# Idle bf16 products on TensorE behind each pair of edge tiles of a two-layer graph attention kernel, with a reordered start, shared edge pools and a different ending

## The chip, the cores and the metric

The kernel runs on one core of a Trainium2 chip. The metric is the time of one execution on the device in microseconds (us). The number to be forecast is the median of several runs of the changed kernel; the kernel before has a median of 2784.78 us.

## What is computed

The reference is a graph network with 6250 nodes and 100000 edges, which come sorted by destination. Cut to what matters:

```python
h = relu(layernorm(x))                      # x: 6250 x 768, no scale and shift
h = relu(gat(h, W1, heads=4))               # 768 -> 4 x 64
h = relu(gat(h, W2, heads=1))               # 256 -> 256
h = relu(h @ Wm1 + bm1)                     # 256 -> 256
out = x + h @ Wm2 + bm2                     # 256 -> 768

def gat(h, W, heads):                       # edges and one self loop per node
    h = h @ W
    e = leaky_relu((h*a_src).sum()[src] + (h*a_dst).sum()[dst], 0.2)
    w = exp(e - max over the edges of dst)
    return sum over edges of w*h[src]  /  sum over edges of w   (+ bias), by dst
```

## The kernel before

**Stages.** There are 49 node tiles of 128 nodes (the last has 106), and the edges lie in 196 groups of 4 tiles of 128 edges, of which 782 tiles hold edges. The work goes through three stages.

1. *Features* (lines 193 to 273). For each node tile SyncE loads x and its transpose (`fetch`, two transfers of 384 KB), VectorE takes mean and variance (`moments`), TensorE spreads the mean over the array with one float32 product (`spread_means`), VectorE and ScalarE subtract and apply relu (`centre`), TensorE multiplies with W1 in six float32 products (`features1`), and `keep1` writes a row of 264 numbers per node to `table1` in device memory.
2. *Edges of layer 1* (`layer_edges`, line 317). For each tile of 128 edges GpSimd issues an indirect DMA that gathers 128 rows of `table1` into `G` (`gather`, line 339), ten groups ahead, into a pool of twelve groups. `make_mask` compares destination numbers, which `fetch_rows` loads broadcast to all partitions (512 KB per 16 tiles), with the partition number; `meet` multiplies this mask (bf16) with the destination scores (`e_ps`). `pair` then takes two tiles: two exponentials on ScalarE, three or four operations on VectorE that end in `hw`, and two float32 products of 128 x 128 by 128 x 260 (258 in layer 2) on TensorE that sum the edges of a group into a window of 128 destinations (`o_ps`, line 429). `gather_up` adds the window to the running sum `acc`, from which a copy of 32 rows per group fills the sum of a node tile. Once a node tile is full its generator `node.steps` is put on the list `late`, and `advance`, called after each pair, makes one step of it: in layer 1 the division, two transposes, the product with W2 and a row of `table2`.
3. *Edges of layer 2*, the same function with another node program (`Node2.steps`): division, transposes, the product with Wm1, that with Wm2 in two halves (`y_ps`), the sum with x + bm2, and the write of the result.

**Order.** The order of each engine's instructions is that of the program text, since these parts stand in `manual_schedule`. Of the main loop:

```python
for g in range(NG):
    gather(g + AHEAD); pair(g, 0); advance(); make_hot(g + 1)
    ...                                   # join / fetch_rows, meet, make_mask
    pair(g, 1); advance(); gather_up(g - 1)
```

The layers run one after the other: a gather of layer 2 may read any row of `table2`, so the first waits for the last row that layer 1 writes.

**PSUM.** The eight banks hold the counter `iota_ps` (1), tag "e" (2), tag "n" (2) and tag "o" (3, the windows `o_ps`).

**Partial tile.** The last node tile has 106 rows. Its load of x (line 156), its reload in layer 2 (line 608) and its write of the result (line 651) are each one transfer of 106 rows. Line 617 adds bm2, broadcast to all partitions, to x. Lines 455 and 458 copy the last window into the last sum.

Of the kernel before, what the change touches and what calls it, by code (L numbers as in the profile page):

```python
# [17 lines left out]
P = 128  # L18
# [3 lines left out]
HID = 256  # L22
# [25 lines left out]
def kernel(  # L48
# [39 lines left out]
    make_identity(nc, ident)  # L88
    iota = const.tile([P, P], F32, name="iota")
# [18 lines left out]
    for k in range(4):  # L108
        nc.vector.memset(keep[32 * k:32 * k + 32, k:k + 1], 0.0)

# [32 lines left out]
    def scores_in(ps, w, wt, a, K, H):  # L143
        p = ps.tile([P, K, 2 * H], F32, name="aps", tag="e")
        for k in range(K):
            for j in range(KH):
                nc.tensor.matmul(p[:, k], wt[:, j, k * P:(k + 1) * P], a[:, j],
                                 start=(j == 0), stop=(j == KH - 1))
        nc.vector.tensor_copy(w[:, :, HID:], p)

    def load_x(xp, i):
        n = min(P, N - i * P)
        t = xp.tile([P, IN_DIM], F32, name="xt", tag="xt")
        if n < P:
            nc.vector.memset(t, 0.0)
        nc.sync.dma_start(t[:n], x[i * P:i * P + n])
        return t, n
# [4 lines left out]
    def edge_places(ones):  # L162

        dst_i = ones.tile([P, NET], I32, name="dst_i")
        nc.scalar.dma_start(dst_i, dst_cols)
        dri = ones.tile([NCH, CH], I32, name="dri")
        nc.scalar.dma_start(dri, dst_rows)
        nc.scalar.dma_start(src_i, src_cols)
        for layer in bT:
            with nc.allow_non_contiguous_dma(reason="256 numbers"):  # L170
                nc.scalar.dma_start(bT[layer], {1: b1, 2: b2}[layer].rearrange("(k p) -> p k", p=P))
        yield

        drm = ones.tile([NCH, CH], BF16, name="drm")
        for d, n, w, to, f in ((dst_i, P, NET, dcol, dst_f), (dri, NCH, CH, drm, None)):
            m = ones.tile([n, w], I32, name=f"m{n}")
            nc.vector.tensor_scalar(m, d, P - 1, None, ALU.bitwise_and)
            yield
            if f is None:
                f = ones.tile([n, w], F32, name=f"f{n}")  # L180
            nc.vector.tensor_copy(f, d)
            yield
            far = ones.tile([n, w], F32, name=f"far{n}")
            nc.vector.tensor_scalar(far, f, float(N), 256.0, ALU.is_ge, ALU.mult)
            yield
            nc.vector.tensor_add(to, far, m)
            yield
        nc.scalar.dma_start(dmod_d, drm)
# [3 lines left out]
    bT = {layer: const.tile([P, KH], F32, name=f"bT{layer}") for layer in (1, 2)}  # L192
    with tc.tile_pool(name="w1p", bufs=1) as wp, tc.tile_pool(name="x1", bufs=6) as xp, \
            tc.tile_pool(name="wk1", bufs=3) as wk, tc.tile_pool(name="once", bufs=1) as ones, \
            tc.manual_schedule():
        xs, xTs, means, cents, rs = {}, {}, {}, {}, {}

        def fetch(i):
            xs[i], _ = load_x(xp, i)
            xTs[i] = xp.tile([P, KI, P], F32, name="xTt")  # L200
            nc.sync.dma_start(xTs[i], xT[i].rearrange("p (k n) -> p k n", k=KI))

        def moments(i):
            xt = xs.pop(i)
            stats = wk.tile([P, 2, nc.vector.BN_STATS_DIM], F32, name="stats")
            for j in range(2):
                nc.vector.bn_stats(stats[:, j], xt[:, j * 384:(j + 1) * 384])  # L207
            mv = wk.tile([P, 2], F32, name="mv")
            nc.vector.bn_aggr(mv, stats)
            std = wk.tile([P, 1], F32, name="std")  # L210
            nc.scalar.activation(std, mv[:, 1:2], AF.Sqrt, bias=eps_c)
            rstd = wk.tile([P, 1], F32, name="rstd", bufs=4)
            means[i] = mv, std, rstd

        def spread_means(i):
            mv, _, rstd = means[i]
            m_ps = ps.tile([P, P], F32, name="mean_ps", tag="n")
            nc.tensor.matmul(m_ps, mv[:, 0:1].to_broadcast([P, P]), ident, start=True, stop=True)
            means[i] = m_ps, rstd
# [9 lines left out]
        def features1(i):  # L229
            r, rstd = rs.pop(i)  # L230
            h_ps = ps.tile([P, HID + 8], F32, name="h_ps", tag="o", bufs=3)
# [14 lines left out]
        fetch(0)  # L246
        loaded = weights_in(wp, W1T, A1, KI, 4, "w1")
        fetch(1)
        w1 = wp.tile([P, KI, HID + 8], F32, name="w1")
        nc.sync.dma_start(w1[:, :, :HID], W1.rearrange("(k p) f -> p k f", p=P))  # L250
        for i in range(2, 5):
            fetch(i)
        pieces = edge_places(ones)
        next(pieces)
        for i in range(-3, NT):
            if i == 0:
                scores_in(ps, w1, *loaded, KI, 4)
            if 0 <= i:
                if i + 5 < NT:
                    fetch(i + 5)  # L260
                h = features1(i)
            if i + 3 < NT:
                moments(i + 3)
            if 0 <= i + 2 < NT:
                _, std, rstd = means[i + 2]
                nc.vector.reciprocal(rstd, std)
                spread_means(i + 2)
            if 0 <= i + 1 < NT:
                centre(i + 1)
            if 0 <= i:  # L270
                keep1(i, *h)
                if i >= 2:
# [43 lines left out]

    def layer_edges(layer, H, node, pre, matched):
# [3 lines left out]
        with tc.tile_pool(name=f"g{layer}", bufs=AHEAD + 2) as gp, \  # L321
                tc.tile_pool(name=f"rows{layer}", bufs=3) as rows, \
                tc.tile_pool(name=f"eg{layer}", bufs=2) as eg, \
# [3 lines left out]
            G, drow, mask, hot, e_ps, o_ps = {}, {}, {}, {}, {}, {}  # L327
# [5 lines left out]
            def gather(g):  # L333
                if not 0 <= g < NG:
                    return
                G[g] = gp.tile([P, TPG, TW[layer]], F32, name="G")
# [5 lines left out]

            def fetch_rows(r):

                k = 16 * r
                if 0 <= k < NET:
                    drow[r] = rows.tile([P, 16 * P], BF16, name="drow")
                    n = min(16, NET - k) * P
                    nc.sync.dma_start(drow[r][:, :n], bcast(dmod_d, n, k * P))
# [5 lines left out]
            def make_mask(u):  # L355

                if not 0 <= u < NU:
                    return
                a, b = (t * P for t in both(u))
                mask[u] = eg.tile([P, 8 * P], BF16, name="mask")  # L360
                at = u % 2 * 8 * P
                nc.vector.tensor_scalar(mask[u][:, a:b], drow[u // 2][:, at + a:at + b], pidx, None,  # L362
                                        ALU.is_equal)

# [29 lines left out]
            def pair(g, p):  # L394
# [26 lines left out]
                if g not in o_ps:  # L421
                    o_ps[g] = ps.tile([P, RW[layer]], F32, name="o_ps", tag="o", bufs=3)
                for t in range(2):
# [3 lines left out]
                    else:  # L427
                        l, r = hot[g][:, k], hw[:, t].rearrange("p h c -> p (h c)")
                    nc.tensor.matmul(o_ps[g], l, r[:, :RW[layer]], start=(k == tiles(g)[0]),  # L429
                                     stop=(k == TPG - 1))  # L430

            done, run, late = {}, {}, []

            def gather_up(g):
# [3 lines left out]
                acc = sums.tile([P, RW[layer]], F32, name="acc")  # L438
                if g == 0:
                    nc.vector.tensor_copy(acc, o_ps.pop(g))  # L440
                else:
                    nc.vector.scalar_tensor_tensor(acc, run[0], keep[:, (g + 1) % 4:(g + 1) % 4 + 1],  # L442
                                                   o_ps.pop(g), ALU.mult, ALU.add)
                run[0] = acc
                a = g - 2
                if a < 0:
                    return
                t, q = divmod(a, 4)
                if q == 0:
                    done[t] = sums.tile([P, RW[layer]], F32, name="sum", bufs=3)  # L450
                    node.prefetch(t)
                if q == 2:
                    node.ahead(t)
                r = slice(32 * q, 32 * q + 32)
                nc.scalar.activation(done[t][r], acc[r], AF.Copy)  # L455
                if g == NG - 1:
                    node.ahead(t)
                    nc.vector.tensor_copy(done[t][64:], acc[64:])
                    q = 3
                if q == 3:  # L460
                    late.append(node.steps(t, done.pop(t)))
# [7 lines left out]
            for r in range(3):  # L469
                fetch_rows(r)  # L470
            for u in range(2):
                make_mask(u)
# [6 lines left out]
            for g in range(NG):  # L479
# [7 lines left out]
                else:  # L487
                    if g % 4 == 0:
                        fetch_rows(g // 4 + 3)
# [6 lines left out]
                hot.pop(g, None)  # L496
            gather_up(NG - 1)
# [18 lines left out]
    with tc.tile_pool(name="w2p", bufs=1) as wp, tc.tile_pool(name="wk2", bufs=2) as wk:  # L516
        w2 = with_scores(ps, wp, W2, W2T, A2, KH, 1, "w2")

        class Node1:
# [12 lines left out]
            def steps(self, t, sum_):  # L532
# [13 lines left out]
                for k in range(KH):  # L546
                    nc.tensor.matmul(h_ps, rT[:, k], w2[:, k], start=(k == 0), stop=(k == KH - 1))
# [7 lines left out]
        with tc.tile_pool(name="pre1", bufs=1) as pre:  # L555
            pre1 = prepare(pre, 1, 4)
            with tc.manual_schedule():
                layer_edges(1, 4, Node1(), pre1, lambda: None)


    with tc.tile_pool(name="wmp", bufs=1) as wp, tc.tile_pool(name="x3", bufs=3) as xp, \
            tc.tile_pool(name="wk3", bufs=2) as wk, tc.tile_pool(name="pre2", bufs=1) as pre, \
            tc.manual_schedule():
# [3 lines left out]
        bm2b = wp.tile([P, OUT_DIM], F32, name="bm2b")  # L567
# [4 lines left out]
        def matched():  # L572
# [6 lines left out]
            nc.scalar.dma_start(bm2b, bcast(bm2, OUT_DIM))  # L579
# [20 lines left out]
        class Node2:  # L600
            rows, xs = {}, {}

            def prefetch(self, t):
# [4 lines left out]
                nc.sync.dma_start(self.xs[t][0][:n], x[t * P:t * P + n])  # L608
# [6 lines left out]
            def ahead(self, t):  # L615
                xt, n = self.xs[t]
                nc.vector.tensor_add(xt[:n], xt[:n], bm2b[:n])

            def steps(self, t, sum_):
# [23 lines left out]
                for s in range(2):  # L643
                    y_ps[s] = ps.tile([P, half], F32, name="y_ps", tag="n")
                    for j in range(KH):
                        nc.tensor.matmul(y_ps[s], mT[:, j], wm2[:, j, s * half:(s + 1) * half],  # L646
                                         start=(j == 0), stop=(j == KH - 1))
# [3 lines left out]
                nc.sync.dma_start(out[t * P:t * P + n], y[:n].rearrange("p s f -> p (s f)"))  # L651
# [301 lines left out]
```

## Time and profile before

| | us |
|---|---|
| median of 3 runs | 2784.78 (2783.95 to 2788.01) |
| the profiled execution, its own time | 2218.71 |
| its span, first to last instruction | 2216.9 |
| PE (TensorE products) busy | 1581.7 |
| DVE (VectorE) busy | 1480.5 |
| POOL (GpSimd) busy | 1518.4 |
| ACT (ScalarE) busy | 599.4 |
| first gather of layer 1 starts, from the span's start | 187.83 |
| first gather of layer 2 starts | 1186.64 |
| last gather of layer 2 starts | 2184.07 |

Read it so: the profile is of one execution, which was much shorter than the runs that were timed (2218.71 against 2784.78 us); every duration below is of that one execution. A group's line gives line number, engine, operation, output and inputs, count, then busy time, mean ns of one, and the idle time of the engine ahead of it with what ended it. "PEclk" and the clock column are the share of TensorE's full clock that was granted. A float32 product appears as two records.

### The profile page before, as it was taken

Reading aid. Unit: us, or ns where it says so; the run is one execution under the profiler, and the core shown is the slowest. Engines: PE = TensorE matmul, PEld = TensorE weight load, DVE = VectorE, ACT = ScalarE, POOL = GpSimd, SP = SyncE. Lnnn points to the kernel's source line nnn. Section 1 sums busy time; section 2 is a strip of 40 time slices with the busy share of each in tenths; the row PEclk is TensorE's granted clock in tenths of the full one; section 3 lists DMA queues with packets and bytes.
Section 4 is the critical chain, followed back from the end, with each engine's and each line's share of the span. In section 5 each row is a group of like instructions: output and inputs, shape, how many; then the busy total and the mean of one; then the engine's idle time right before and its main releaser. Section 6 shows DMA issues by size and latency. Waiting matters only on the chain. (4 is left out here: it accounts for less than half of the span.)

```text
span 2216.9 us, 25764 instructions
## 1 busy us (share of the span) xinstructions
PE 1581.7 (71%) x6588; PEld 1099.4 (50%) x6589; DVE 1480.5 (67%) x4510; ACT 599.4 (27%) x2602; POOL 1518.4 (68%) x1672
## 2 busy tenths in 40 slices
PE   7995766676667676666675777677877777777776
PEld 6783444444444444444443455555555554555553
DVE  6665677777777677777775666666666666666663
ACT  3552222222222222222222222222222222222221
POOL 0004777777777777777775777777777777777773
PEclk9997777877887877887886798888777878778786
DMA  8893555555555555545545565565556556555652
GB/s 288 291 306 109 143 145 151 151 139 148 152 152 141 146 151 151 150 139 150 151 122 172 162 182 158 183 182 165 177 181 182 166 174 183 171 166 182 181 143 89
DMA packets 149839, 370.16 MB, mean 167 GB/s; under 512 B 34354, under 2 KB 60978, under 8 KB 149684
## 3 DMA queue, kind: packets, MB, share of 16 engines
q0 software_dynamic: 75072, 209.10, 35.0%
q1 hardware_dynamic: 72052, 156.47, 21.3%
q10 hardware_dynamic: 2560, 2.86, 0.4%
q8 instruction: 56, 0.92, 0.2%
q14 instruction: 99, 0.81, 0.1%
HBM read 335.80 MB, written 32.50 MB: 166 GB/s over the span
## 5 line engine op out<-in xcount | busy, mean ns | idle before, releaser
L339 POOL DMA_INDIRECT G<-table,src_i x1564 | 1504.4, 962 | 496.1 <-issue 404.8
L429 PE MATMUL o_ps<-hw,hot 128*128 128x260 f32 x1564 | 590.8, 514 | 319.0 <-DVE hw L418 310.9
L429 PE MATMUL o_ps<-G,hw 128*128 128x258 f32 x1564 | 564.2, 497 | 260.2 <-DVE hw L413 255.9
L429 PEld LDWEIGHTS o_ps<-hw,hot 128*128 128x128 f32 x1564 | 345.1, 244 | 503.8 <-DVE hw L418 436.2
L429 PEld LDWEIGHTS o_ps<-G,hw 128*128 128x128 f32 x1564 | 339.2, 238 | 425.5 <-DVE hw L413 371.7
L406 DVE TENSOR_TENSOR e_ps<-e,e_ps 128x8 f32<-128x8 f32 (+1 forms) x782 | 129.6, 166 | 550.9 <-ACT e L403 550.8
L455 ACT ACTIVATE sum<-acc 32x260 f32<-32x260 f32 (+1 forms) x388 | 161.7, 417 | 696.7 <-DVE acc L442 695.5
L413 DVE TENSOR_SCALAR hw<-iota_ps,dcol,w 128x128 f32<-128x128 f32 x782 | 285.0, 406 | 14.4
L401 ACT ACTIVATE e<-G 128x8 f32<-128x8 f32 (+1 forms) x782 | 158.9, 203 | 471.1 <-DMA G<-table,src_i 452.1
L418 DVE TENSOR_TENSOR hw<-G,e_ps 128x520 f32<-128x520 f32 x391 | 271.8, 695 | 14.5 <-DVE e_ps L416 1.2
L442 DVE SCALAR_TENSOR_TENSOR acc<-acc,keep,o_ps 128x260 f32<-128x260 f32 (+1 forms) x390 | 185.7, 476 | 3.3 <-PE o_ps L429 3.3
L233 PE MATMUL h_ps<-w,r 128*128 128x264 f32 x588 | 146.5, 401 | 13.2 <-ACT r L226 13.1
L403 ACT ACTIVATE e<-G 128x8 f32<-128x8 f32 (+1 forms) x782 | 150.0, 192 | 0.2
L646 PE MATMUL y_ps<-wm,mT 128*128 128x384 f32 x392 | 143.1, 488 | 1.3 <-ACT mT L640 0.9
L372 DVE TENSOR_TENSOR hot<-iota_ps,dcol 128x512 f32<-128x512 f32 (+1 forms) x196 | 133.8, 682 | 0.0
L233 PEld LDWEIGHTS h_ps<-w,r 128*128 128x128 f32 x588 | 112.2, 197 | 33.5 <-ACT r L226 15.5
L243 POOL COPY row<-sd 128x4 f32<-128x4 f32 x49 | 9.1, 186 | 170.0 <-ACT sd L242 170.0
L512 ACT ACTIVATE rT<-tp,bT 128x128 f32<-128x128 f32 x196 | 61.2, 363 | 159.6 <-PE tp L505 159.3
L362 DVE TENSOR_SCALAR mask<-drow,pidx 128x1024 bf16<-128x1024 bf16 (+1 forms) x196 | 96.4, 493 | 2.2 <-DMA drow<-dmod_d 2.2
L383 PEld LDWEIGHTS <-mask 128*128 128x128 bf16 x1564 | 73.3, 101 | 42.6 <-issue 18.4
L646 PEld LDWEIGHTS y_ps<-wm,mT 128*128 128x128 f32 x392 | 74.2, 190 | 34.1 <-ACT mT L640 1.4
L207 DVE BATCH_NORM_STATS2 stats<-xt 128x6 f32<-128x384 f32 x98 | 49.9, 551 | 51.0 <-DMA xt<-in_x 50.4
(385 smaller groups left out, 1091.4 us busy)
## 6 DMA issues: line engine op xcount, KB each, us to landing
drow<-dmod_d SPq DMA_DIRECT2D x98, 512.0 KB, 5.6
xt<-in_x SPq DMA_DIRECT2D x96, 384.0 KB, 4.2
G<-table,src_i POOLq DMA_INDIRECT x1564, 2.8
xTt<-in_xT SPq DMA_DIRECT2D x49, 384.0 KB, 4.7
out<-y SPq DMA_DIRECT2D x48, 384.0 KB, 3.3
table<-row SPq DMA_DIRECT2D x49, 132.0 KB, 3.5
row<-table SPq DMA_DIRECT2D x49, 130.0 KB, 5.6
table<-row SPq DMA_DIRECT2D x49, 129.0 KB, 2.8
```

What stands on the lines that cost most here:

```text
L233: nc.tensor.matmul(h_ps, r[:, k], w1[:, k], start=(k == 0), stop=(k == KI - 1))
L339: nc.gpsimd.indirect_dma_start(out=G[g][:, t], out_offset=None, in_=table[layer], in_offset=bass.IndirectOffsetOnAxis(ap=src_i[:, k:k + 1] ...
L372: nc.vector.tensor_tensor(hot[g][:, T[0]:T[0] + n], iota_ps.unsqueeze(1).to_broadcast([P, n, P]), dcol[:, k:k + n].unsqueeze(2).to_broadca ...
L401: nc.scalar.activation(e1, sc, AF.Exp)
L403: nc.scalar.activation(e2, sc, AF.Exp, scale=SLOPE)
L406: nc.vector.tensor_mul(v, e2, rho)
L413: nc.vector.tensor_scalar(hw[:, t], iota_ps, dcol[:, k:k + 1], w[:, t], ALU.is_equal, ALU.mult)
L418: nc.vector.tensor_mul(hw, G[g][:, T, :RW[1]].rearrange("p t (h c) -> p t h c", h=H), w.unsqueeze(3).to_broadcast([P, 2, H, C + 1]))
L429: nc.tensor.matmul(o_ps[g], l, r[:, :RW[layer]], start=(k == tiles(g)[0]), stop=(k == TPG - 1))
L442: nc.vector.scalar_tensor_tensor(acc, run[0], keep[:, (g + 1) % 4:(g + 1) % 4 + 1], o_ps.pop(g), ALU.mult, ALU.add)
L455: nc.scalar.activation(done[t][r], acc[r], AF.Copy)
L646: nc.tensor.matmul(y_ps[s], mT[:, j], wm2[:, j, s * half:(s + 1) * half], start=(j == 0), stop=(j == KH - 1))
```

## The change

The new kernel differs in these things:

- **Idle products.** Behind each pair's two float32 products, `stay_awake` issues products of a zero bf16 tile, 128 x 128 by 128 x 512, into a PSUM bank of their own that nothing reads: four per pair in layer 1, two in layer 2, none in the last three groups of either layer. In the built program there are 385 such pairs per layer, so 1540 and 770 products.
- **PSUM.** The bank for them comes from tag "o", which now has two windows instead of three.
- **Start.** The scores of W1 are taken before the first tile's features, the loads are put in another order, the edge lists are loaded piece by piece on SyncE between node tiles instead of all at once on ScalarE's queue, and from the third node tile on the mean is spread as three bf16 products of its parts instead of a float32 one, with five small GpSimd operations per tile that make the parts.
- **Between the layers.** One manual schedule and one set of edge pools spans both layers. W2's scores are taken after layer 1's first gathers are issued. Layer 1 writes each mask (256 KB) to device memory; layer 2 loads it instead of the 512 KB of destination numbers, and compares nothing. The last window goes to the last node tile without the copies.
- **End.** bm2 is added by a bf16 product with three rows in `y_ps` instead of VectorE's addition, and the last node tile's transfers are split into 96 and 10 rows, its result by halves as well.

```diff
+    idle = const.tile([P, 4 * P], BF16, name="idle")
+    nc.vector.memset(idle, 0.0)
+    idle_ps = ps.tile([P, 4 * P], F32, name="idle_ps", bufs=1)
+
+    def stay_awake(n):
+        for _ in range(n):
+            nc.tensor.matmul(idle_ps, idle[:, :P], idle, start=True, stop=True)
...
+    def runs(n):
+
+        return [(a, b) for a, b in ((0, n // 16 * 16), (n // 16 * 16, n)) if a < b]
...
-        nc.sync.dma_start(t[:n], x[i * P:i * P + n])
+        for a, b in runs(n):
+            nc.sync.dma_start(t[a:b], x[i * P + a:i * P + b])
...
+                for k in range(3):
+                    nc.tensor.matmul(m_ps, parts[:, k:k + 1].to_broadcast([P, P]), ident_b,
+                                     start=(k == 0), stop=(k == 2))
...
+                if layer == 2:
+                    return fetch_mask(u + 1)
...
+                nc.sync.dma_start(mask_d[u * P:(u + 1) * P], mask[u])
...
-                    o_ps[g] = ps.tile([P, RW[layer]], F32, name="o_ps", tag="o", bufs=3)
+                    o_ps[g] = ps.tile([P, RW[layer]], F32, name="o_ps", tag="o")
...
+                if g < NG - 3:
+                    stay_awake(4 if layer == 1 else 2)
...
+                last = g == NG - 1
...
+                if last:
+
+                    late.append(node.steps(t, acc))
...
+                if layer == 1 and g == NG - 3:
+                    for k in range(3):
+                        fetch_mask(k)
...
             def ahead(self, t):
-                xt, n = self.xs[t]
-                nc.vector.tensor_add(xt[:n], xt[:n], bm2b[:n])
+                pass
...
+                    nc.tensor.matmul(y_ps[s], ones_r, bm2r[:, s * half:(s + 1) * half],
+                                     start=True, stop=False)
...
+                    if t == NT - 1:
+                        for a, b in runs(n):
+                            nc.sync.dma_start(out[t * P + a:t * P + b, s * half:(s + 1) * half],
+                                              y[a:b, s])
```

## The prediction

> **What bounds the kernel now.** I read the stages first, cut at the first and last gather of each layer (start, length, then busy time of PE, weight loads, DVE, ACT and POOL, granted clock, DMA share, GB/s):
>
> ```profile
> 0.00:187.80 187.80, 158.68 (x718) 134.60 (x719) 112.75 (x274) 87.19 (x202) 13.95 (x108) 0.97 0.80 271
> 187.80:1169.60 981.80, 658.19 (x2620) 431.51 (x2620) 708.80 (x1995) 239.46 (x1162) 743.88 (x782) 0.79 0.53 145
> 1169.60:1186.60 17.00, 9.01 (x36) 5.50 (x34) 9.92 (x35) 5.30 (x17) 0.05 (x1) 0.60 0.54 155
> 1186.60:2185.00 998.40, 739.71 (x3168) 517.57 (x3168) 640.47 (x2186) 262.20 (x1204) 760.48 (x782) 0.80 0.58 173
> 2185.00:2216.80 31.80, 16.07 (x48) 10.25 (x48) 8.55 (x23) 5.25 (x17) 0.01 (x1) 0.66 0.11 39
> ```
>
> The two edge stages are 1980 of 2217 us, and in each POOL issues 782 gathers: 981.8/782 = 1.256 and 998.4/782 = 1.277 us each. The groups of instructions show why:
>
> ```profile
> L339 POOL DMA_INDIRECT G<-table,src_i x1564 | 1504.4, 962 | 496.1 <-issue 404.8
> L429 PE MATMUL o_ps<-hw,hot 128*128 128x260 f32 x1564 | 590.8, 514 | 319.0 <-DVE hw L418 310.9
> ```
>
> A gather is 0.96 us and the idle time ahead of it is mostly its own issue, about 0.3 us. Nothing downstream holds it up: POOL is its own bound there, while PE waits for `hw`, which waits for gathered rows. TensorE's granted clock is 0.79, and the order of time shows what that means (start, duration):
>
> ```profile
> 603.19 1.23 PE L429 MATMUL o_ps<-hw,hot 128*128 128x260 f32 x4 [2.40 <-DVE hw L418]
> ```
> ```profile
> 526.34 2.10 PE L429 MATMUL o_ps<-hw,hot 128*128 128x260 f32 x4 [0.21 <-DVE hw L418]
> ```
>
> The same four records take 1.23 us at one time and 2.10 at another; the second lies in a stretch with a granted clock of 0.50. The slow ones still fit: a pair has 2 x 1.25 = 2.50 us. Three waits outside the gathers matter too:
>
> ```profile
> 169.61 1.02 DVE L207 BATCH_NORM_STATS2 stats<-xt 128x6 f32<-128x384 f32 x2 [6.99 <-DMA xt<-in_x]
> ```
> ```profile
> 1186.64 0.94 POOL L339 DMA_INDIRECT G<-table,src_i  x1 [17.00 <-DMA drow<-dmod_d]
> ```
> ```profile
> 2206.08 0.27 SPq L651 DMA_DIRECT2D out<-y  x1
> ```
>
> The 106-row load keeps DVE idle for 6.99 us; the layers are 17.00 us apart; and the span ends 10.8 us after the last 106-row write is issued.
>
> **The gap.** The median, 2784.78, is 1.255 times the profiled execution's own 2218.71 (span 2216.9 and 1.8 around it). No view shows those 566 us, so what stretches the timed runs is the largest unknown here.
>
> [...] 10.8 us for 106 rows, where a full `out` takes 3.3 in the list of issues. [...]
>
> **The change part by part**, against the profiled execution.
>
> *Idle products.* [...] Do they fit under the gathers? Per pair of layer 1 at full clock: pair 1.14 us (a later row of the same kind), masks 0.1, an eighth of a node tile's transposes and W2 product (0.44 + 1.14)/8 = 0.2[...]. Layer 2: 1.14, 0.1, an eighth of the node program (0.44, 1.05 for Wm1, 2.85 for Wm2: 0.54)[...]. [...] Queued behind them on PE are the next pair's products and node steps[...]; behind those wait DVE's `acc` and ACT's copies. The gather pool runs ten groups (50 us) ahead, which hides this. Taken: 0. If the clock stays at 0.50 the cover is gone (rival C).
>
> *Two windows instead of three* for `o_ps`: a window is needed again only after `gather_up` of two groups earlier, which DVE runs behind the same pair. Bounds 0 to 0.48 us (one `acc` operation) per group, hidden in the 5 us of a group: 0.
>
> *Masks through memory.* Layer 2 loses 97 comparisons x 0.49 = 48 us of DVE and 25 MB of broadcasts, and gains 25 MB of mask loads; layer 1 gains 25 MB of writes, 98 more SP issues of about 0.35 us. DMA is at 0.53 in layer 1 and 0.58 in layer 2, so both are hidden. On SP a mask write waits for its comparison, and row loads and table writes queue behind it; they are a node tile ahead. 0, bounds -5 to +10 us.
>
> *Start.* The split load removes most of DVE's 6.99 us wait: -5. From 120 to 150 us DMA is 94% and PE 95% busy, so neither the three bf16 products for one float32[...] nor the paced edge lists shorten a tile; POOL's five small operations have 2.5 us of idle time per tile. The first products start at 19.6 us; scores taken earlier may save 2 to 5, of which the DMA bound leaves about 2. W2's scores leave the way of the first gather: -1. Sum -8, bounds -14 to +2.
>
> *Between the layers.* The last `table2` row is issued at 1180.77 and the first gather starts 5.9 us later; such a row lands in 2.8 us in the list of issues when no 512 KB broadcasts stand ahead of it. -3. The copies on lines 455 and 458 go: -0.7; three 256 KB masks now stand ahead of it: +0.7. Sum -3, bounds -6 to +3.
>
> *End.* The last write falls from 10.8 to about 3.3 us: -7.5. Lines 458 and 617 (0.29 + 0.95 of DVE) go, two small bf16 products come: -0.5. Sum -8, bounds -11 to -5.
>
> Together -8 - 3 - 8 = -19: the profiled execution falls to about 2200 us. The parts that shrink are waits for DMA and issue, and whatever stretches the timed runs by 1.255 should leave them between 19 and 24 us. I take -22: 2784.8 - 22 = 2763 us.
>
> **The rivals.**
>
> *A, gathers set the pace in the timed runs too* (0.50): 2763, own range 2740 to 2785. For it: POOL's step is regular, no engine it depends on is full, and 566 us over 1564 gathers is 0.36 us each, as a slower POOL would give. Against: nothing shows such a POOL.
>
> *B, the timed runs are slow because TensorE's clock sleeps there* (0.22), and the idle products wake it. Then the time falls to what the profiled execution gives: about 2200, or up to 2650 if it wakes in part. For it: PE is next in line. Against: at half clock I get only layer 2 over the pace: pair 2.2, masks and node program 0.1 + 7.0/8, 3.1 us per pair, 240 us over the layer, with some 100 in the start; that doesn't reach 566.
>
> *C, PE becomes the bound* (0.22), slower. [...] For it: the products are heavy and in PE's order. Against: busier windows have woken the clock in this trace.
>
> *D, nothing measurable* (0.06): the savings outside the gathers are given back.
>
> **How the numbers follow.** Likeliest is A, 2763 us. A measurement of this kernel can tell about 0.2% (5.6 us) from no change. Faster: A with 0.46 and B with 0.22, so 0.68; same: 0.04 of A and D, 0.10; slower: C, 0.22. For 8 in 10 the range takes A, D, B from 2180 and the mild end of C up to 2850; the rest of C is left out.
>
> **What would show it.** Right: gathers still at 1.25 us, layers of about 982 and 990 us, a clock near 1.00 in both, first gather near 180, a layer gap of about 14, and an end within 4 us of the last write. Wrong: PE over 95% busy in an edge stage with gathers waiting for `hw` or `o_ps` (C); or a median that closes on the profiled time (B), which would mean that the gap was TensorE's clock.

## The result, and the profile after

The changed kernel takes 2781.34 us (median of 4 runs, 2776.61 to 2783.83), the kernel before 2784.36 us in the same comparison: a ratio of 0.999, 95% interval 0.9966 to 1.0013. The forecast of 2763 us, 0.8% faster, was wrong: no difference can be measured. That 2781 us lies inside the stated range says little, since the range ran from 2180 to 2850 us so as to hold rivals A, B and D and a part of C.

To read what follows: runs made together always fell into one and the same of two regimes, "with stalls", where the kernel before takes 2720 to 2785 us and its engines stand still for about 450 us inside the layers, and "without stalls", where it takes 2220 us; the execution profiled before was of the second, the timed runs of the first.

The stages of the changed kernel, cut at the first and last gather of each layer (columns as in the prediction's first view: start and length; busy time of PE, weight loads, DVE, ACT, POOL; granted clock; DMA share; GB/s):

```profile
0.00:176.40 176.40, 154.18 (x757) 126.88 (x758) 112.67 (x274) 86.86 (x200) 60.94 (x344) 0.99 0.82 275
176.40:1454.00 1277.60, 890.37 (x3883) 535.32 (x3958) 675.98 (x1899) 215.88 (x1099) 751.06 (x782) 0.85 0.46 132
1454.00:1515.80 61.80, 50.29 (x238) 31.17 (x240) 43.79 (x129) 16.81 (x80) 0.03 (x1) 0.94 0.18 52
1515.80:2716.30 1200.50, 855.14 (x3802) 532.77 (x3868) 538.61 (x1954) 239.59 (x1150) 742.23 (x782) 0.87 0.48 143
2716.30:2782.10 65.80, 48.99 (x225) 30.81 (x226) 33.08 (x114) 15.73 (x70) 0.04 (x1) 0.95 0.17 56
```

POOL is busy for 751 us of 1278 in layer 1. No other engine is full either (PE 890). Some of the costliest groups:

```profile
L411 POOL DMA_INDIRECT G<-table,src_i x1564 | 1493.4, 955 | 1049.2 <-issue 882.6
L498 PE MATMUL o_ps<-hw,hot 128*128 128x260 f32 x1564 | 494.2, 442 | 341.9 <-DVE hw L487 291.6
L120 PE MATMUL idle_ps<-idle 128*128 128x512 bf16 x2161 | 654.1, 409 | 16.2 <-issue 8.6
```

A gather is still 955 ns and the median step from one to the next still 1.254 us. But the idle time ahead of gathers is 1049 us where it was 496: 187 steps inside the layers are longer than 2 us and hold 500 us more than 1.254 each; another 62 and 66 us pass between the layers and at the end, where it was 17 and 32. The stalls recur with the node tile, every sixteen gathers: about two long steps per tile in either layer (89 and 98 steps for 49 tiles). One of them, in the order of time (start, duration; idle time and what ended it in brackets):

```profile
595.55 0.35 PE L452 MATMUL e_ps<-win,mask 128*128 128x12 bf16 x8
...
600.22 0.38 PE L580 MATMUL tp<-ident,o 128*128 128x128 f32 x2
...
601.99 0.95 POOL L411 DMA_INDIRECT G<-table,src_i  x1 [0.30 <-issue]
...
605.23 0.27 DVE L459 TENSOR_REDUCE e_ps<-e_ps 128x32 f32<-128x96 f32 x1 [5.27 <-remote]
...
605.43 0.63 ACT L587 ACTIVATE rT<-tp,bT 128x128 f32<-128x128 f32 x2 [8.05 <-remote]
...
607.24 0.95 POOL L411 DMA_INDIRECT G<-table,src_i  x1 [4.30 <-issue]
```

The mask products end at 595.90 us, and the reduction that reads them starts at 605.23; the transposes end at 600.60, and the `rT` that reads them starts at 605.43. From 600.60 on nothing but gathers runs. Both waits are for TensorE's semaphore, which 1420 of its products in this trace raise and no other engine does. The trace holds three updates of it in one burst, at 605.20, 605.26 and 605.40, the first and last of which end the two waits; in order they belong to products that had ended 9.3, 8.0 and 4.8 us earlier (by order only: the trace lacks some of the updates, as is told below). Meanwhile POOL issues gathers until its twelve buffers are used up (the last starts at 601.99), and the next one has to wait until the work on rows gathered earlier goes on. "remote" is the profile's word for a wait that it can lay at no instruction's end. In the list of waits such holds are among the largest items:

```profile
POOL G L411 <- issue: 882.6, 1476, 13.1
ACT sum L526 <- DVE acc L515: 712.3, 202, 57.2
ACT rT L587 <- remote: 411.5, 57, 15.1
...
DVE e_ps L459 <- remote: 284.1, 58, 41.9
```

The columns are total, number of waits and the longest. The 500 us inside the layers and the longer stretches behind them are about what the prediction called "the gap", 566 us. Are these holds the change's, or were they in the timed runs of before as well?

### The profile page after: what moved, and what is told of

It is laid out like the page before. It is cut to its first block, busy times and chain, and to the rows that moved or that the text cites. A ratio compares the mean times of both kernels' runs of the same rounds, so it can differ in the third digit from the quotient of the medians.

```text
span 2782.1 us, 30999 instructions
## 1 busy us (share of the span) xinstructions
PE 1999.0 (72%) x8894; PEld 1256.9 (45%) x9044; DVE 1404.1 (50%) x4369; ACT 574.9 (21%) x2598; POOL 1554.3 (56%) x1908
## 3 DMA queue, kind: packets, MB, share of 16 engines
q8 instruction: 76, 1.25, 0.2%
## 4 chain that ended last, share of the span: by engine, by line
DVE 27%; PE 24%; issue 18%; another core or an unknown queue 18%; ACT 6%; DMA 4%; POOL 3%; SPq 0%; ACTq 0%; POOLq 0%; DVEq 0%
PE o_ps L498 10%; DVE hw L487 8%; PE idle_ps L120 4%; PE y_ps L724 4%; DVE hw L482 4%; ACT sum L526 3%; DVE acc L515 3%; DVE e_ps L475 3%; POOL G L411 2%; PE h_ps L291 2%; DMA G<-table,src_i 2%; DVE e_ps L485 2%; ACT e L470 1%; PE m_ps L711 1%
## 5 line engine op out<-in xcount | busy, mean ns | idle before, releaser
L498 PE MATMUL o_ps<-hw,hot 128*128 128x260 f32 x1564 | 494.2, 442 | 341.9 <-DVE hw L487 291.6
L498 PE MATMUL o_ps<-G,hw 128*128 128x258 f32 x1564 | 480.9, 435 | 277.4 <-DVE hw L482 167.9
L120 PE MATMUL idle_ps<-idle 128*128 128x512 bf16 x2161 | 654.1, 409 | 16.2 <-issue 8.6
L498 PEld LDWEIGHTS o_ps<-hw,hot 128*128 128x128 f32 x1564 | 301.0, 211 | 489.1 <-DVE hw L487 360.9
L498 PEld LDWEIGHTS o_ps<-G,hw 128*128 128x128 f32 x1564 | 300.4, 208 | 418.9 <-DVE hw L482 236.2
L120 PEld LDWEIGHTS <-idle 128*128 128x128 bf16 x2310 | 241.5, 105 | 252.7 <-issue 65.0
L459 DVE TENSOR_REDUCE e_ps<-e_ps 128x32 f32<-128x96 f32 (+2 forms) x196 | 43.4, 222 | 351.1 <-remote 284.1
L724 PE MATMUL y_ps<-wm,mT 128*128 128x384 f32 x392 | 165.3, 547 | 39.8 <-ACT mT L716 29.4
L728 DVE TENSOR_TENSOR y<-y_ps,xt 128x384 f32<-128x384 f32 (+1 forms) x98 | 52.4, 553 | 129.1 <-PE y_ps L724 58.5
```

The lines of the kernel that those rows point to most:

```text
L120: nc.tensor.matmul(idle_ps, idle[:, :P], idle, start=True, stop=True)
```

## The experiments

Steps, stage lengths and stalls are of the one profiled execution of each run; "stalls" is what the steps over 2 us between gathers hold beyond the median step, inside the layers (the texts on record, written ahead of the runs, count the stretch between the layers in: 563 us for the changed kernel). In the texts of e1 to e4, S is a stall of the whole core and "Rival P" is the clock, the prediction's rival B; from e5 on P is another theory, named below. Ratios are to the kernel before, run beside each, whose median is given.

**e1, the kernel before once more**, unchanged.

> The kernel before, unchanged, for a profile of an execution that takes as long as the timed ones. In the profile of the changed kernel all engines stand still together about once per node tile (16 gathers) for 4 to 5 us, and GpSimd's gathers have 188 steps of over 2 us that hold 563 us beyond their 1.25 us. Theory S (a stall of the whole core, which has nothing to do with TensorE's clock or with the change, makes the 566 us): about 2784 us, and its gathers show gaps of 500 to 600 us in sum while the rest of the steps stay at 1.25 us. Rival P (TensorE at half clock is what makes the timed runs slow): about 2784 us, gathers with steps that are all longer (1.6 us), and a mean clock near 0.5. Third: it takes 2219 us as the first profile did, and then the stall belongs to the changed kernel alone.

Measured: 2769.38 us (before: 2779.13). Its stages:

```profile
0.00:184.00 184.00, 156.13 (x718) 132.82 (x719) 112.95 (x274) 87.23 (x202) 14.14 (x109) 0.99 0.82 277
184.00:1425.50 1241.50, 674.01 (x2477) 428.94 (x2478) 667.42 (x1885) 209.72 (x1095) 752.10 (x782) 0.72 0.41 114
1425.50:1489.90 64.40, 41.95 (x178) 27.32 (x178) 48.35 (x144) 18.14 (x85) 0.01 (x2) 0.82 0.20 54
1489.90:2689.80 1199.90, 716.82 (x3016) 487.13 (x3016) 601.84 (x2077) 238.93 (x1142) 761.18 (x782) 0.82 0.47 142
2689.80:2767.60 77.80, 51.49 (x200) 34.00 (x200) 39.90 (x131) 18.10 (x79) 0.01 (x1) 0.81 0.14 47
```

The kernel before has the same stalls: 451 us of them, with a median step of 1.251 us. The timed runs are slow because the core stands still, not because gathers are slower: the median step is 1.251 us in the first profile too. So the slower POOL that rival A allowed for is not what stretches them. The stretches between the layers and at the end are longer too, 64.4 and 77.8 us against 17.0 and 31.8 in the first profile.

**e4, the idle products alone**: the kernel before with them and with two `o_ps` windows.

```diff
+    def stay_awake(n):
+        for _ in range(n):
+            nc.tensor.matmul(idle_ps, idle[:, :P], idle, start=True, stop=True)
...
-                    o_ps[g] = ps.tile([P, RW[layer]], F32, name="o_ps", tag="o", bufs=3)
+                    o_ps[g] = ps.tile([P, RW[layer]], F32, name="o_ps", tag="o", bufs=2)
...
+                if g < NG - 3:
+                    stay_awake(4 if layer == 1 else 2)
```

> The kernel before with only the idle products and the bank that they need (two windows instead of three). Theory S: 2784 us within 0.5%, so that the products are hidden here too. Rival P: a large fall, towards 2219 us. Rival C: a rise of over 1%.

Measured: 2782.01 us, ratio 1.0006 (0.9989 to 1.0022). The granted clock in 40 slices of the span (tenths), e1 first, then e4:

```profile
PEclk9985776777777777667677588888888888888888
```
```profile
PEclk9985888898887889888898699898998989999999
```

The idle products do wake the clock, from a mean of 0.783 to 0.880, and the time of the kernel before doesn't move. Rival B is out.

**e2, the change without its idle products**, that is without the call of `stay_awake`.

> The changed kernel without its idle products; all other edits stay. Theory S: the idle products cost and bring nothing, 2781 us within 0.5%. Rival P: without them the clock sleeps again and the time rises. Rival C (the products fill TensorE and cost time that the other edits win back): it falls to about 2600 us or less.

Measured: 2803.81 us, ratio 1.0087 (1.0067 to 1.0107). So with stalls the other edits together cost 0.9%, and with the idle products added nothing is left of that. In the profile it is layer 1 that is longer: 1300 us, against 1278 with them and 1242 in e1.

**e3, slower gathers**: the changed kernel with `nc.gpsimd.memset(pool_rest, 0.0)`, 128x64, behind every gather.

> The changed kernel with one memset of 128 x 64 float32 on GpSimd behind each gather, so that a gather's step rises from 1.25 to about 1.4 us. Theory S in the form that the stalls come when gathers run at full pace and end when their traffic pauses: fewer or shorter stalls, and the kernel gets faster although its pacing engine has more to do, 1564 x 1.4 + 240 = 2430 us at best. If the stalls come from something else, once per node tile of their own: they stay at 5.8 us per node tile and the time rises by 1564 x 0.15 = 235 us less what the stalls hide, 2800 to 3000 us.

Measured: 2769.21 us, ratio 0.9967 (0.9951 to 0.9982), at a step of 1.281 us; stalls 439 us. The changed kernel's step is 1.254 us, so the gathers are slower by 0.027 us each, 42 us in all, and the kernel is no slower. Rival A, for which every gather counts, fails here. The step grew much less than the expected 0.15 us, so that this run alone says little about a rest between gathers.

That left three theories of the stalls, which the next texts call P (something else serves a node tile in about 25 us whatever the gathers do), T (a burst of transfers per node tile triggers them) and N (the node tile's own chain is the cause).

**e5, a pause of 0.4 us** behind every gather: the memset 128x512.

> The changed kernel with a memset of 128x512 on GpSimd behind every gather; the step from gather to gather should grow from 1.25 us to about 1.5. Sixteen gathers (one node tile) then take 24 us by themselves, against the 25.4 us that a node tile takes now with its stall. Theory P (something other than the gathers serves a node tile in 24.5 to 26 us, the stall is only what is left over): the stalls shrink from about 560 us to 100 to 200 us and the time stays within 1% of before, near 2780 us. Theory T (a burst of transfers at each node tile holds the core up for some 6 us, whatever the gathers do): the stalls stay near 560 us and the time grows by 1564 x 0.25 = 390 us, to about 3170 us.

Measured: 2829.97 us, ratio 1.0396 (1.0368 to 1.0425; before: 2721.97). The step is 1.656 us and the stalls are gone:

```profile
POOL G L413 <- issue: 248.0, 1491, 0.5
```

The longest wait of POOL for its issue is 0.5 us, where it was 13.1; 2 us of stalls are left of some 500, and 15.3 and 24.0 us between the layers and at the end. T, with 3170 us, is wrong. P's time, within 1% of before, is missed as well, but the step grew more than expected: sixteen gathers take 26.5 us by themselves, longer than P's own 24.5 to 26, so P stays possible.

**e6, no bursts of 512 KB**, and **e7, more packets.**

```diff
+        if r >= 3:
+            drow[r] = drow[r % 3]
-        if r < NET // 16:
+        elif r < NET // 16:
```
```diff
...
+                            nc.sync.dma_start(extra[:, :, :16],
+                                              x[:P, :128].rearrange("p (a b) -> p a b", b=32)[:, :, :16])
```

> The changed kernel, in which layer 1 loads only its first three strips of destination rows (drow, 512 KB each) and uses them again, so that 46 of the 49 loads of 512 KB are left out (the masks are then wrong in content, not in shape). Layer 2 is untouched and serves as the control. Theory T: the burst that starts the stall is gone, layer 1 shortens from 1278 us towards its 49 x 20 = 980 us, the kernel to about 2500 us. Theory P with a pace set by transfers: layer 1 shortens in proportion to its packets or bytes, some 50 to 150 us. Theory N (the node tile's own chain of transposes is the cause): no change, within 1% of 2780 us.

> The changed kernel with one more transfer per node tile and layer on SyncE: 512 packets of 64 B (32 KB) from the input x to a tile that nobody reads. Theory P with a pace set by the number of packets (about 1400 per node tile of 26 us in layer 1): 512 more make a node tile 5 to 9 us longer, the kernel some 400 us or more, about 3200 us. Theory P with a pace set by bytes, theory T and theory N: at most 2 us per node tile, 2780 to 2880 us.

Measured: e6 2740.83 us, ratio 1.006 (1.0036 to 1.0084); e7 2740.85 us, ratio 1.008 (1.0049 to 1.0111); before: 2721.97. Layer 1 takes 1251 us without the bursts and 1246 us with the bursts and 512 packets more per node tile, with 450 and 442 us of stalls in the whole kernel. The changed kernel as it is was not run beside them, so the two are compared with each other; neither the bursts nor the number of packets sets the stalls.

**e8, no transposes and products in layer 1's node step.**

```diff
-                p = turn(o)
...
-                rT = straighten(wk, 1, p)
-                h_ps = ps.tile([P, HID + 2], F32, name="h_ps", tag="n")
-                for k in range(KH):
-                    nc.tensor.matmul(h_ps, rT[:, k], w2[0][:, k], start=(k == 0), stop=(k == KH - 1))
...
```

> The changed kernel whose layer 1 leaves out, in the step of a node tile, the two transposes, the two rT and the two products with W2 (the row of layer 2 is the quotient itself), so that only DVE, one copy on ACT and the write are left. Layer 2 is untouched and serves as the control. Theory N: layer 1 loses its stalls and shortens from 1278 us towards 980 us, the kernel to about 2500 us. Theories P and T: the stall goes to the next wait, layer 1 stays within 3% of 1278 us and the kernel within 1.5% of 2780 us.

Measured: 2836.04 us, ratio 1.0389 (1.0344 to 1.0433). With less work on TensorE layer 1 grows to 1363 us. N is wrong. P gave at most 1.5% and has no place for this either. Why less work makes it longer stays open; e2 shows the same direction.

**e9 to e12, other pauses, in both kernels.** The same memset, 128x256 (e9) and 128x352 (e10) in the changed kernel, 128x352 (e11) and 128x512 (e12) in the kernel before. G is a new theory: gathers without rest make the stalls.

> The changed kernel with a memset of 128x256 on GpSimd behind every gather; from the widths tried (64: 172 ns, 512: 544 ns, steps 1.281 and 1.656 us) the step should be about 1.44 us, 23.1 us for sixteen gathers. Theory P (something serves a node tile in 24.2 to 25.6 us whatever the gathers do): the layers stay at 1180 to 1280 us each, with stalls of some 150 us left, the kernel within 1% of the kernel before. Theory G (the stalls come from gathers that follow each other without a rest; with enough rest they are gone): stalls below 50 us, layers of 49 x 23.1 = 1132 us each, gap and tail as at 1.656 us (15 and 24 us), the kernel about 2480 us by its profile, 0.90 to 0.93 of before.

> The same with a memset of 128x352: step about 1.52 us, 24.4 us for sixteen gathers. Theory P: layer 1 1250 us, layer 2 1195 us, the stalls nearly gone, gap and tail perhaps at 15 and 24 us (then 90 us are won there): 0.96 to 1.00 of before. Theory G: no stalls, layers of 1194 us each, gap 15, tail 24: about 2600 us by its profile, 0.94 to 0.96 of before.

> The kernel before with the same memset of 128x352 behind every gather. If the stalls are gone in both, what the change saves outside the gathers (the start, the end, the stretch between the layers, 19 us by the prediction) comes to light: the kernel before then takes 10 to 25 us longer than the changed one at the same pace. If the change were worth nothing even without stalls, the two agree within 5 us. If stalls are left, the pair says nothing on this.

> The kernel before with the memset of 128x512 that the changed kernel had at 1.656 us per gather, where that one had no stalls (ratio to before 1.040). Prediction's sum right: head about 184 against 173 us, end about 32 against 24 us, both layers the same within 5 us, a ratio of 1.045 to 1.05. Sum wrong: a ratio of 1.04 or less.

Measured: these runs fell into the regime without stalls; the kernel before took 2220.16 us beside them. The ratios are 1.1258 (1.1239 to 1.1277), 1.1803 (1.1783 to 1.1823), 1.1969 (1.1949 to 1.1989) and 1.2839 (1.2817 to 1.286). So P and G aren't told apart here, and e12's expected ratios, made for the other regime, say nothing. But e10 and e11 are the clean pair that the prediction's sum asked for: the same pace, no stalls. The kernel before, then the changed one:

```profile
0.00:187.60 187.60, 158.54 (x718) 135.21 (x719) 112.92 (x272) 87.13 (x202) 14.01 (x108) 0.97 0.81 271
187.60:1394.90 1207.30, 735.90 (x2621) 495.48 (x2621) 737.47 (x1998) 252.39 (x1162) 1076.22 (x1563) 0.71 0.44 118
1394.90:1411.70 16.80, 8.15 (x34) 5.48 (x34) 9.37 (x33) 5.31 (x17) 0.45 (x2) 0.70 0.51 156
1411.70:2624.90 1213.20, 774.31 (x3168) 521.56 (x3168) 645.53 (x2185) 272.59 (x1204) 1081.71 (x1563) 0.77 0.48 143
2624.90:2656.40 31.50, 16.56 (x48) 10.27 (x48) 8.74 (x24) 5.14 (x17) 0.44 (x2) 0.66 0.10 34
```
```profile
0.00:174.60 174.60, 154.21 (x757) 126.73 (x758) 112.42 (x274) 86.87 (x200) 60.74 (x345) 0.99 0.83 278
174.60:1381.90 1207.30, 899.50 (x4091) 555.28 (x4168) 730.76 (x2005) 253.68 (x1164) 1076.20 (x1563) 0.89 0.50 142
1381.90:1397.10 15.20, 8.30 (x30) 5.14 (x31) 6.79 (x25) 4.36 (x15) 0.44 (x3) 0.59 0.18 35
1397.10:2592.80 1195.70, 887.72 (x3974) 565.23 (x4043) 567.53 (x2054) 274.68 (x1207) 1063.82 (x1563) 0.90 0.49 146
2592.80:2618.00 25.20, 15.78 (x48) 9.36 (x48) 5.71 (x16) 3.60 (x12) 0.42 (x2) 0.70 0.13 38
```

Start -13.0, layer 1 0.0, between -1.6, layer 2 -17.5, end -6.3: 38.4 us less, and the medians (2657.9 and 2619.57 us) say 38.3. Without stalls the change is worth 1.4% at this pace, more than the 10 to 25 us that were expected. A second pair without stalls, at 1.656 us per gather, is e12 (2851.0 us) and e5 (2829.97 us, from another set): 21.0 us less, near the prediction's 19. The changed kernel without a pause was never run in the regime without stalls, so what the change is worth there is not measured.

**e13 to e16, back with stalls.** The changed kernel again (e13), with the 128x256 pause (e14), without idle products (e15), and the kernel before with the same pause (e16). The same chip as in e9 to e12 now gave the other regime (before: 2773.05 us), so what the texts call a chip with or without stalls is a regime, not a chip.

> The changed kernel, unchanged. On a chip where the kernel before takes about 2220 us: the prediction's sum gives 19 us less, a ratio of 0.991; from the paced pair (2618.0 against 2656.4 us by the profiles) up to 38 us less, 0.983. If the idle products cost time at full pace, the ratio is above that. On a chip where the kernel before takes about 2780 us: 0.995 to 1.003 as measured, with stalls of about 560 us.

> The changed kernel with a memset of 128x256 behind every gather (step 1.443 us, 2498 us on a chip without stalls). On a chip without stalls: 1.126 of before again. On a chip with stalls, theory P: layers of 1180 to 1280 us with stalls of some 150 us, 0.97 to 1.00 of before; theory G: stalls below 50 us, about 2500 us, 0.90 to 0.92 of before.

> The changed kernel without its 2310 idle products. On a chip without stalls: if the idle products are hidden under the gathers, as the prediction had it, the same within 0.2% as the changed kernel; if they cost or save time, the difference to it is their price. On a chip with stalls: 1.0 to 1.4% above the changed kernel, as before (1.0087 against 0.999).

> The kernel before with the memset of 128x256 behind every gather. On a chip without stalls: 28 to 38 us above the changed kernel at the same pace (2498 us), as the pairs at 1.523 and 1.656 us showed. On a chip with stalls, theory P: 0.97 to 1.00 of before; theory G: about 2530 us, 0.91 to 0.93.

Measured: e13 2773.38 us, 1.0004 (0.9985 to 1.0022); e14 2647.84 us, 0.9543 (0.9513 to 0.9573); e15 2802.14 us, 1.0099 (1.0078 to 1.0121); e16 2560.13 us, 0.9227 (0.9204 to 0.925). e13 and e15 repeat the result and e2. e14 and e16 beat both kernels although each gather is issued later, since the steps over 2 us now hold only 69 and 30 us. Of e16's 30, 26.5 are no stalls at all: they are 43 gathers of layer 2 that overlap an addition on VectorE and take longer (see below), so that about 4 us are left. The edge stages and the two stretches behind them of e16:

```profile
186.00:1342.80 1156.80, 705.60 (x2620) 469.62 (x2620) 722.68 (x1998) 251.30 (x1162) 1025.20 (x1563) 0.73 0.45 123
1342.80:1359.50 16.70, 9.66 (x34) 6.08 (x34) 9.38 (x33) 5.31 (x17) 0.35 (x2) 0.50 0.55 156
1359.50:2529.00 1169.50, 769.05 (x3168) 519.97 (x3168) 642.67 (x2187) 274.43 (x1204) 1037.80 (x1563) 0.77 0.50 148
2529.00:2561.60 32.60, 17.42 (x48) 10.57 (x48) 8.68 (x23) 5.14 (x17) 0.38 (x2) 0.66 0.10 34
```

A node tile takes 23.7 us in layer 1, less than the 25.4 us of e1, although POOL does more. So nothing serves a node tile at a fixed rate: P is wrong. For the kernel before G's forecast came true (0.91 to 0.93, stalls below 50 us). For the changed kernel neither did: 0.9543 lies between G's 0.92 and P's 0.97, and e14 keeps 59.3 us between the layers and 64.8 us at the end, where e16 has 16.7 and 32.6. That a rest takes the stalls away is thus shown for the kernel before, and by e5, with the longer pause, for the changed one; how it does so is not.

**e17 and e18**: the kernel before with half the rest (128x160), and e14 without idle products.

> The kernel before with a memset of 128x160 behind every gather: step about 1.36 us, 21.8 us for sixteen gathers. Theory G with a threshold below 1.36 us: stalls below 60 us, about 2430 us, 0.88 of before. Theory P in the form that a call's stalls fill up what a slower gather leaves: the time stays where 1.447 us put it or above, 2560 us or more, 0.92 or more. If the kernel before takes about 2220 us in this call (no stalls): 2430 us, 1.09.

> The changed kernel without idle products, with the memset of 128x256 (step 1.443 us). If the 2310 idle products are what keeps the stalls in the changed kernel: gap and tail fall from 59 and 65 us to about 15 and 25 us, stalls to 30 us, 0.92 of before or less. If it is the masks through memory (or anything else): gap, tail and stalls stay, 0.95 to 0.97 of before. If the kernel before takes about 2220 us in this call (no stalls): 2498 us as with them, 1.125.

Measured: without stalls again (before: 2221.63 us), e17 2413.75 us, 1.0855 (1.083 to 1.0879), e18 2503.53 us, 1.126 (1.1239 to 1.1281). What keeps the holds in e14 is thus not settled, nor how little rest is enough. e18 gives something else: it stands beside e9, the same with idle products, at 1.1258 of its own before. Without stalls, at that pace, the idle products cost nothing that can be measured.

## Why the prediction was wrong

*The failed step* is the last of its sum: "whatever stretches the timed runs by 1.255 should leave them between 19 and 24 us". It took the stretching as something that leaves the savings outside the gathers as they are. Two executions of nearly the same length show where they went:

| us | before (e1) | changed (e13) | difference |
|---|---|---|---|
| start | 184.0 | 175.4 | -8.6 |
| layer 1 | 1241.5 | 1273.4 | +31.9 |
| between | 64.4 | 62.6 | -1.8 |
| layer 2 | 1199.9 | 1190.0 | -9.9 |
| end | 77.8 | 66.5 | -11.3 |
| span | 2767.6 | 2767.9 | +0.3 |

Start, between and end save 8.6 + 1.8 + 11.3 = 21.7 us, where the prediction had 19, stretched to 22. That the sums agree so well is partly luck, since the last two stretches are themselves some 46 us longer each than without stalls. Layer 1 eats the saving: its stalls are 282 us against 251 in e1. These are single executions, and runs of one kernel in one set differ by up to 32 us (e4), but the other profiles with stalls have the same sign: layer 1 takes 1277.6 us in the first profile of the changed kernel, and 1253.1 in e4, the kernel before with idle products. So the stretching is no factor on the parts that are there. It is holds, and their sum changes with the kernel by as much as was saved. Which of the edits adds to them in layer 1 is not shown.

By its other steps:

- *Idle products, 0.* Right without stalls at the pace tried (e18 against e9), and with stalls for the kernel before (e4: 1.0006). In the changed kernel with stalls they are worth -1% (e13 against e15), which no step had. PE is at 890 of 1278 us in layer 1, idle products included (654.1 us for the 2161 recorded in both layers): they fit, and rival C did not come. Ahead of the result that they fit, and how far C goes, was the author's estimate, since no row of before shows such a product.
- *The clock near 1.00.* 0.85 and 0.87 in the edge stages, higher than before but not full; in the kernel before a rise from 0.783 to 0.880 had no effect on the time (e4). That busy stretches precede a rise is in the first profile of before: PE is busy for 95% of the 4 us ahead of the clock's 109 rises from 0.50 to 1.00, and for 42% ahead of its 110 falls (means).
- *Two windows, 0.* Within e4's interval, together with the idle products.
- *bm2 by a product instead of an addition*, which the prediction counted once, at the end, with line 617's 0.95 us. Mis-sized: this addition stands in each of layer 2's 49 node tiles, and gathers that overlap it take longer. In the kernel before at the paced rate (e11, its line 619), on POOL and on DVE:

```profile
1497.82 0.95 POOL L340 DMA_INDIRECT G<-table,src_i  x1 [0.16 <-issue]
...
1499.34 1.20 POOL L340 DMA_INDIRECT G<-table,src_i  x1 [0.17 <-issue]
...
1501.12 0.95 POOL L340 DMA_INDIRECT G<-table,src_i  x1 [0.17 <-issue]
```
```profile
1498.77 0.95 DVE L619 TENSOR_TENSOR xt<-xt,bm2b 128x768 f32<-128x768 f32 x1
```

  The gather that starts while the addition runs takes 1.20 us instead of 0.95. In this trace 53 gathers overlap an addition, at a mean of 1.215 us, 14.0 us above the median together: most of the 17.5 us by which the changed kernel's layer 2 is shorter. (All gathers of layer 2 together lie 19.5 us above it in e11 and 2.7 in e10.) What the gather waits for inside is not shown. How much is met depends on the pace: the same sum is 9.3 us in the first profile of before, 7.3 in e1, 26.8 in e16 and 2.0 in e12. No kernel changed this addition alone.
- *Masks through memory, 0, bounds -5 to +10.* Without stalls 17.5 - 14.0 = 3.5 us of saving are left for it in layer 2 and 0.0 in layer 1: inside the bounds. Most of the 3.5 is again shorter gathers: in e11 the 88 gathers of layer 2 that start during a mask comparison, which the changed kernel doesn't make there, lie 2.7 us above the median together. In the first profile of before these are 64 gathers and 9.6 us, as much as the additions cost there. With stalls the edits other than the idle products lengthen layer 1 to 1300 us (e2), and of these the mask writes are the largest there; but they were not taken away by themselves, so that this is argued, not shown.
- *Start -8, between -3, end -8.* -13.0, -1.6 and -6.3 in the clean pair, -8.6, -1.8 and -11.3 with stalls. Each lies within its bounds but the last, which just passes -11. That 96 and 10 rows land sooner than 106 in one transfer was the author's estimate; between the first profiles of the two kernels DVE's wait for the load falls from 6.99 to 0.55 us, and the span ends 5.6 us after the last write is issued instead of 10.8.
- *Rival D, "the savings outside the gathers are given back"*, is what happened with stalls; it had 0.06. The first profile could not show it, since it held none of the 566 us. That the median was 1.255 times the profiled time was a reason not to forecast by its stages. Of the signs named ahead, gathers at 1.25 us came true and no sign of B or C appeared, but the layers of 982 and 990 us, the gap of 14 and the short end did not come: the list of signs had none for holds.

What the holds are is open. They come and go with the regime, in which the recording of events fares differently as well: the trace of the kernel before holds 1381 updates of TensorE's semaphore in its first profile and 1379 to 1384 in e11, e12 and e17, but 1089 in e1 and 1105 in e16, which has next to no stalls; the first profile of the changed kernel holds 1267, fewer than the 1420 products in it that raise it. So records are lost in this regime even where next to nothing is held. Every run with a trace was by nature recorded, so no run tells a hold of the core from one of its recorder. It would be no matter of the mere number of records either: e16 has 1564 instructions more than e1 and is 206 us shorter.

## What to carry to other kernels

When the profiled execution and the median differ by a quarter, first profile an execution of the median's length: a sum made by stages of the other holds for that other one alone. If all engines idle once per period while every instruction is as fast as ever, it is worth trying a short rest in the producer that runs ahead: a step longer by 0.2 us per gather took 7.7% off the kernel before where it stalls (e16). Where it doesn't stall, the changed kernel with the same pause is at 1.126 of the kernel before (e9), so know the regime first. A higher clock on an engine that isn't on the path bought nothing (e4: 0.783 to 0.880, at a ratio of 1.0006). And what VectorE does can lengthen the gathers that GpSimd issues (e11: from 0.95 to 1.2 us), so an operation taken off VectorE may pay on another engine.

## What the runs showed of the hardware

- One program on one chip took 2220 us in one set of runs and 2773 us in another, each steady within about 1%. The profiles of the two regimes have the same median gather, 0.946 us in the first profile of before and 0.947 in e1.
- In the stall shown, instructions that waited for products of TensorE started up to 9.3 us after the product had ended, several at once and after the gathers had stopped. A step longer by 0.2 us from gather to gather took the long steps from 451 us to 30 in the kernel before, of which 26.5 are gathers that overlap the additions (e1, e16).
- With stalls, less work made the changed kernel slower: without idle products by 1.0% (e15 against e13), and without layer 1's node products, and the copies on ScalarE that go with them, it is at 1.039 of the kernel before (e8). In the kernel before, idle products made no difference (e4: 1.0006).
- The gathers on GpSimd that overlap an addition of two 128x768 f32 tiles in SBUF on VectorE take 1.2 us on average in e11 and 1.5 us in e16, where the median gather takes 0.95.
